# First attention of a four-layer graph stack: scores computed once, products transposed on TensorE

## The chip, the cores and the metric

The kernel runs on one core of a Trainium2 chip. The metric is the time of one execution on the device, in microseconds (us). A core has five engines with a queue each that works strictly in order: PE (TensorE, matrix products; its weight loads are listed as PEld), DVE (VectorE), ACT (ScalarE), POOL (GpSimd) and SP (SyncE, which here only issues DMAs). The engines wait for one another through semaphores. PE writes to PSUM, a memory of banks of 128 partitions x 512 f32.

## The reference

There are 64 independent batch elements, each with `x` (256 nodes x 128 features) and `adj` (256 x 256, some 6% of it nonzero, with the diagonal). Four layers follow one another, each `x = x + layer(relu(layernorm(x)), adj)`: an attention with 8 heads, a one-head graph attention, two graph attention layers with 4 heads each, and a layer that sends a message over every pair of nodes. The change is in the first:

```python
q, k, v = (heads of h @ W.T + b)                    # 8 heads of 16 columns
scores = einsum('bhnd,bhmd->bhnm', q, k) / sqrt(HD)
scores = where(adj == 0, -inf, scores)
attn = softmax(scores, axis=-1) * adj
attn = attn / (attn.sum(-1) + 1e-08)
ctx = einsum('bhnm,bhmd->bhnd', attn, v)            # then @ Wo.T + bo
```

With e = exp(score - row maximum), a context row is sum(e * adj * v) / (sum(e * adj) + 1e-8 * sum(e)). Both kernels compute this form.

## The kernel before

All 64 elements pass through one straight program. Nodes are cut into NB = 2 blocks of 128. The work on an element is split into eight streams, Python generators named by a letter: `f` (`first`: loads, layer norm, the first attention `mha`), `m` (`marks`: masks and ranks), `s` (`second`: the one-head attention and one `gat`), `t` (`third`: the other `gat`), `l` (`lists`: sorted neighbour lists), `e` (`edges`), `g` (`weigh`) and `u` (`fourth`). Each `yield` ends a turn. The string `ORDER` is one round: its letters say which stream takes the next turn. A stream has as many letters in a round as it has turns in an element, so that one round moves every stream on by one element; `START` says by how many rounds and letters a stream lags. In one round the streams thus work on different elements, and the table alone fixes the order of the instructions in every engine's queue. `NBATCH + 9` rounds are run.

Inside `mha`, heads are numbered h = 4a + r with a in 0, 1 and r in 0..3. Head r of group a lies in partitions 32r to 32r + 31 of `qT[:, a]` and `kT[:, a]`: row 0 of the 32 is a spare one, rows 1 to 16 are the head. A product of one head so uses 32 rows of PE, and products of different r can run side by side. The steps of `mha` in the kernel before:

- `qT`, `kT` and values are projected (PE) and copied with bias (ACT, and DVE for the values `va`).
- First pass, queries on partitions: for each block nb and each pair of r, two PSUM banks (from `bank()`, which hands out four) get the mask (`ident_n`, minus 1e30 on its diagonal, times the 0/1 mask) and the scores of two values of a. DVE reduces each bank to row maxima `mx_p` (L468).
- The maxima are transposed by PE (L474), and DVE adds them to the spare rows of `qT` (L476); the spare rows of `kT` hold -1, so that a product is score minus maximum.
- Second pass, keys on partitions: the same products again with swapped operands and the transposed mask; ACT takes the exponential from PSUM to `e` (L491), POOL multiplies by `adT`, the transposed adjacency, into `ew` (L497).
- PE sums over keys into `pc`: `va` (ones and values) by `ew`, and `tiny` (1e-8 in one column) by `e` for the small term. ACT copies `pc` (L511), PE transposes it (L517), DVE divides (L521, L525), and the output projection follows.

Helper `mm` records its products at L408, so its rows are told apart by tiles. In the profile, `ps<-kT,qT` is a product of the first pass and `ps<-qT,kT` one of the second (the moving operand stands first); an f32 product is two MATMUL records, an f32 transpose one. The transposes of the two `gat` stages (L688) are four to a bank, followed by DVE work. The `weigh` stream switches ACT's function table to Gelu and back three times an element (L1020, L1025), the `lists` stream to the square root once (L924, L926).

Of the kernel before, what the change touches and what calls it, by code (L numbers as in the profile page):

```python
# [8 lines left out]
F32 = mybir.dt.float32  # L9
# [27 lines left out]


ORDER = (
    "sggtseffffgegeululeellgfgfggsgltflgfuflfssulfsgulslglfflltgtfgtllggeslgelflslgssglggsflsflftffffssss"  # L40
    "slltllffetefesltstfftllslmeessetftetttgsssftfsefssmffeltutfleselftssfsteeftlffemsustsftmgfslftteggff"
    "tllflflgltlllgfftegfsffesllggmsegfmsleeettfssglgsgllgllletlffsegetfsfttsefffffsfftlsegletlltslselels"
    "tmmllslggugltstgugssuetlgeesgsfllellleellseeusltetlelgggggglstuslstflftslflullsllfgsgsgmfsflllllllll"
    "ltssfgftssffsglllllutlemflg"
)

START = {"f": (0, 17), "s": (1, 17), "t": (2, 9), "l": (3, 29), "e": (5, 1), "u": (6, 11), "g": (5, 23), "m": (0, 0)}
EPS = 1e-5
SLOPE = 0.2
BIG = 1e30  # L50
# [3 lines left out]
def listed_pairs(  # L54
# [82 lines left out]
    V.tensor_copy(ident_b, ident)  # L137
    ident_n = const.tile([P, P], BF16, tag="ident_n", name="ident_n")
    V.tensor_scalar(ident_n, ident, -BIG, None, op0=ALU.mult)
    ones = ct([P, N], "ones")  # L140
    V.memset(ones, 1.0)
    ones_b = const.tile([P, P], BF16, tag="ones_b", name="ones_b")
# [29 lines left out]
        return t, c  # L172

    wq_p, bq_p = by_heads(Wq, bq, 0.0, "wq")
    wk_p, bk_p = by_heads(Wk, bk, -1.0, "wk")
    V.tensor_scalar(bq_p, bq_p, HD ** -0.5, None, op0=ALU.mult)
    wv_t, wo_t = load_t(Wv, "wv"), load_t(Wo, "wo")

    va = ct([P, NB, HEADS, 32], "va")
    V.memset(va, 0.0)  # L180
    V.memset(va[:, :, :, 0:1], 1.0)
    tiny = ct([P, 32], "tiny")
    V.memset(tiny, 0.0)
    V.memset(tiny[:, 0:1], 1e-8)
    mx_p = ct([P, NB, HG, RG, 32], "mx_p")
    V.memset(mx_p, 0.0)
    bv_r, bo_r = load_row(bv, "bv"), load_row(bo, "bo")

    key = const.tile([P, N], I32, tag="key", name="key")
# [228 lines left out]
            mm(p[:, nb, :], hT[:, nb * P:(nb + 1) * P], w)  # L418
        return p

    def mha(hT, adT, xt, mask, maskT, st):


        qT, kT = wt([P, HG, N], "qT", st), wt([P, HG, N], "kT", st)
        p = pt().rearrange("p (a n) -> p a n", a=HG)
        for a in range(HG):
            mm(p[:, a], wq_p[:, a], hT)
        yield
        for a in range(HG):
            S.activation(qT[:, a], p[:, a], AF.Identity, scale=HD ** -0.5, bias=bq_p[:, a:a + 1])  # L430
# [24 lines left out]
        def head(t, r, a, nb=None):  # L455
            return t[32 * r:32 * (r + 1), a, :] if nb is None else t[32 * r:32 * (r + 1), a, nb * P:(nb + 1) * P]

        for nb in range(NB):
            for r in range(0, RG, 2):
                ps = [bank() for _ in range(2)]  # L460
                for j in range(2):
                    mm(ps[j], ident_n, mask[:, nb:nb + 1, :].to_broadcast([P, HG, N]), stop=False)
                for a in range(HG):
                    for j in range(2):
                        mm(ps[j][:, a], head(qT, r + j, a, nb), head(kT, r + j, a), start=False, stop=a == HG - 1)
                yield
                for j in range(2):
                    V.tensor_reduce(mx_p[:, nb, :, r + j, 0], ps[j], axis=AX.X, op=ALU.max)  # L468
                    done("ps")
                    yield  # L470
        pm = pt().rearrange("p (a n) -> p a n", a=HG)
        for nb in range(NB):
            for a in range(HG):
                T.transpose(pm[:, a, nb * P:(nb + 1) * P], mx_p[:, nb, a].rearrange("p r c -> p (r c)"), ident)  # L474
        yield
        V.tensor_tensor(qT, qT, pm, op=ALU.add)  # L476
        done()
        yield
        cn = wt([P, HG, N], "cn", st)
        for nb in range(NB):  # L480
            e = big.tile([P, RG, HG, N], F32, tag="e", name="e", bufs=1)
            for r in range(0, RG, 2):
                ps = [bank() for _ in range(2)]
                for j in range(2):
                    mm(ps[j], ident_n, maskT[:, nb:nb + 1, :].to_broadcast([P, HG, N]), stop=False)
                for a in range(HG):
                    for j in range(2):
                        mm(ps[j][:, a], head(kT, r + j, a, nb), head(qT, r + j, a), start=False, stop=a == HG - 1)
                yield
                for j in range(2):  # L490
                    S.activation(e[:, r + j], ps[j], AF.Exp)  # L491
                    done("ps")
                    yield
            yield
            ew = big.tile([P, RG, HG, N], F32, tag="ew", name="ew", bufs=1)
            for r in range(RG):
                G.tensor_tensor(ew[:, r], e[:, r], adT[:, nb:nb + 1, :].to_broadcast([P, HG, N]), op=ALU.mult)  # L497
                yield
            yield
            if nb == 0:  # L500
                pc = pt("pc").rearrange("p (a n) -> p a n", a=HG)
            for a in range(HG):
                for r in range(RG):
                    mm(pc[32 * r:32 * (r + 1), a, :], tiny, e[:, r, a, :], start=a == 0 and nb == 0, stop=False)
            for a in range(HG):
                for r in range(RG):
                    mm(pc[32 * r:32 * (r + 1), a, :], va[:, nb, a * RG + r, :], ew[:, r, a, :],
                       start=False, stop=a == HG - 1 and nb == NB - 1)
            yield
# [218 lines left out]
    def first(b):  # L728

        xt, ad, adT = x1_[b % 3], ad_[b % 2], adT_[b % 2]  # L730
        if b:
            yield from load_element(b)
        else:
            yield
        if b == min(1, NBATCH - 1):
            for nb in range(NB):
                nc.sync.dma_start(eye_v[:, nb, :], bass.AP(adj.tensor, adj[0].offset + nb * P * (N + 1),
                                                           [[N + 1, P], [N * N, NBATCH], [1, 1]]))
        yield
# [9 lines left out]
        yield from mha(hT, adT, xt, off_[b % 3], offT_[b % 3], "0")  # L749

    def marks(b):

# [958 lines left out]
```

## Time and profile before

| | |
|---|---|
| median of 3 runs | 4637.73 us (4633.71 to 4638.06) |
| profiled execution | 4635.24 us |
| its span (first to last instruction) | 4633.5 us |
| PE busy | 4327.5 us, 93% |
| PE weight loads busy | 2565.2 us, 55% |
| DVE busy | 4027.0 us, 87% |
| ACT busy | 3560.6 us, 77% |
| POOL busy | 2692.4 us, 58% |
| granted PE clock | 0.974 of full speed, mean |

The busy time of an engine is the union of its instructions, in the whole span; the first and last 200 us, in which the streams start and run out, are in it. A row of the groups gives the count, the busy time (union) and the mean duration of one instruction. Where instructions of one engine overlap, busy time divided by count is smaller than the mean duration.

### The profile page before, as it was taken

The numbers are of one execution on the slowest core, as the hardware profiler recorded it, in microseconds if no ns is written. First come the engines' busy times: TensorE is split into PE (matmuls) and PEld (weight loads), VectorE is DVE, ScalarE is ACT, GpSimd is POOL, SyncE is SP. The second block draws the span as 40 slices with busy tenths as digits, with TensorE's granted clock in tenths as the row PEclk, the third lists the DMA queues.
The fourth block names the chain that finished last, engine by engine and source line by source line (L and its number), as shares of the span: only waits on it lengthen the run. The fifth ranks groups of instructions, "written<-read, shape, count | busy, mean of one in ns | idle before, by whom it ended". The sixth has DMA issues, their size and how long they took to land. (4 is left out here: it accounts for less than half of the span.)

```text
span 4633.5 us, 90265 instructions
## 1 busy us (share of the span) xinstructions
PE 4327.5 (93%) x30293; PEld 2565.2 (55%) x30293; DVE 4027.0 (87%) x11727; ACT 3560.6 (77%) x7303; POOL 2692.4 (58%) x3210
## 2 busy tenths in 40 slices
PE   7889999999999999999999999999999999999975
PEld 4455555555555555555555555555555555555543
DVE  4688998998998998898998998998898898898984
ACT  3467878878877878878877877877877877887864
POOL 3345655655665665665665665665665665665644
PEclk8899999999999999999999999999999999999987
DMA  1023444444444444444444444444444443444455
GB/s 27 17 84 114 121 119 119 122 122 117 122 123 116 122 121 118 124 121 117 123 121 117 125 118 116 126 118 115 127 122 111 126 123 110 126 123 110 128 140 134
DMA packets 783433, 533.36 MB, mean 115 GB/s; under 512 B 505321, under 2 KB 678510, under 8 KB 782958
## 3 DMA queue, kind: packets, MB, share of 16 engines
q1 hardware_dynamic: 754286, 493.91, 39.3%
q0 software_dynamic: 28672, 33.58, 3.0%
q8 instruction: 241, 3.95, 0.3%
q14 instruction: 234, 1.92, 0.1%
HBM read 479.47 MB, written 47.84 MB: 114 GB/s over the span
## 5 line engine op out<-in xcount | busy, mean ns | idle before, releaser
L1031 POOL TENSOR_TENSOR ms<-ms,wb 128x512 f32<-128x512 f32 x640 | 832.8, 1401 | 930.3 <-ACT ms L1023 909.3
L497 POOL TENSOR_TENSOR ew<-e,adT 128x512 f32<-128x512 f32 x512 | 639.7, 1268 | 167.6 <-ACT e L491 167.1
L412 PE MATMUL up<-oh,cj 128*128 128x512 f16 x2560 | 658.9, 389 | 22.1 <-DVE oh L982 17.0
L408 PE MATMUL agg<-ms,w2b 128*128 128x256 f32 (+2 forms) x2432 | 650.9, 390 | 12.5 <-POOL ms L1031 12.4
L890 DVE MAX8 best<-pl 128x8 f32<-128x256 f32 x1536 | 620.7, 418 | 16.1
L1006 DVE TENSOR_TENSOR ms<-up,rb 128x512 f32<-128x512 f32 x640 | 434.3, 679 | 187.5 <-PE up L412 133.8
L408 PEld LDWEIGHTS agg<-ms,w2b 128*128 128x128 f32 x2432 | 411.9, 192 | 146.4 <-issue 101.6
L893 DVE MATCH_REPLACE8 pl<-best,pl 128x256 f32<-128x256 f32 x1152 | 470.2, 408 | 0.0
L661 ACT ACTIVATE ps<-ps 128x512 f32<-128x512 f32 x512 | 291.2, 597 | 186.5 <-PE ps L408 186.5
L994 ACT ACTIVATE up<-ci 128x512 f32<-128x512 f32 (+6 forms) x896 | 423.8, 478 | 8.1
L1023 ACT ACTIVATE ms<-ms,be,g 128x1024 f32<-128x1024 f32 x320 | 393.8, 1231 | 14.2 <-DVE ms L1006 13.7
L412 PEld LDWEIGHTS <-cj 128*128 128x128 f16 x2560 | 248.5, 99 | 265.4 <-issue 38.7
L468 DVE TENSOR_REDUCE mx_p<-ps 128x2 f32<-128x512 f32 x512 | 337.8, 682 | 55.4 <-PE ps L408 55.4
L408 PE MATMUL ps<-off,ident_n 128*128 128x512 bf16 x1024 | 318.5, 383 | 40.2 <-DVE mx_p L468 32.6
L670 ACT ACTIVATE y<-ps 128x512 f32<-128x512 f32 x512 | 277.3, 596 | 99.3 <-PE ps L412 99.3
L635 DVE TENSOR_REDUCE m<-ps 128x2 f32<-128x512 f32 x512 | 337.9, 681 | 10.6 <-PE ps L408 10.2
L491 ACT ACTIVATE e<-ps 128x512 f32<-128x512 f32 x512 | 277.7, 594 | 83.0 <-PE ps L408 81.1
L982 DVE TENSOR_SCALAR oh<-cb,code 128x1024 f16<-128x1024 f16 x640 | 337.7, 569 | 0.0
L374 POOL TENSOR_SCALAR rs<-mv 128x2 f32<-128x2 f32 x256 | 79.1, 309 | 410.0 <-DVE mv L367 399.8
L408 PE MATMUL ps<-qT,kT 32*128 32x256 f32 x2048 | 291.9, 402 | 5.8 <-DVE qT L476 1.8
L408 PE MATMUL ps<-kT,qT 32*128 32x256 f32 x2048 | 293.7, 404 | 0.0
L408 PEld LDWEIGHTS ps<-kT,qT 32*128 32x128 f32 x2048 | 176.7, 186 | 165.5 <-issue 151.3
(298 smaller groups left out, 10146.4 us busy)
## 6 DMA issues: line engine op xcount, KB each, us to landing
rb<-ws_d SPq DMA_DIRECT2D x256, 512.0 KB
wb<-ws_d SPq DMA_DIRECT2D x256, 512.0 KB
cb<-code_d SPq DMA_DIRECT2D x256, 256.0 KB
ad<-in_adj_dram SPq DMA_DIRECT2D x64, 256.0 KB
adr<-adr_d SPq DMA_DIRECT2D x64, 256.0 KB
rb<-ws_d SPq DMA_DIRECT2D x64, 168.0 KB
wb<-ws_d SPq DMA_DIRECT2D x64, 168.0 KB
x<-in_x_dram SPq DMA_DIRECT2D x64, 128.0 KB
```

The source lines that it names most:

```text
L408: return T.matmul(o, lhsT=lhsT, rhs=rhs, start=start, stop=stop)
L412: return T.matmul(o, lhsT=lhsT, rhs=rhs, start=False, stop=False, skip_group_check=True)
L468: V.tensor_reduce(mx_p[:, nb, :, r + j, 0], ps[j], axis=AX.X, op=ALU.max)
L497: G.tensor_tensor(ew[:, r], e[:, r], adT[:, nb:nb + 1, :].to_broadcast([P, HG, N]), op=ALU.mult)
L635: V.tensor_reduce(m[:, k + j], ps[j], axis=AX.X, op=ALU.max)
L890: V.max(best[:, n, nb, r:r + 8], planes[n][:, nb])
L893: V.match_replace(planes[n][:, nb], best[:, n, nb, r:r + 8], planes[n][:, nb], 0.0)
L982: V.tensor_scalar(oh[:, jb], cb, code[:, jb:jb + 1], None, op0=ALU.is_equal)
L994: S.activation(ps[:, lo - h * 512:hi - h * 512].rearrange("p (k n) -> p k n", n=cap), ci_[v][:, None, :cap].to_broadcast([P, (hi - lo) // ...
L1006: V.tensor_tensor(ms[:, hs], halves[h], rb[:, hs], op=ALU.mult)
L1023: S.activation(parts[b, c], parts[b, c], AF.Gelu, bias=be1_c, scale=g1_c)
L1031: G.tensor_tensor(ms[:, hs], ms[:, hs], wb[:, hs], op=ALU.mult)
```

## The change

The scores are computed once, with queries on partitions, and negated: `qT` is scaled by -1/sqrt(HD), and the mask is added with `ident_p` (plus 1e30). The row minimum of the negated scores is then the negated maximum, and goes straight into the exponential as its bias: exp(-1 * ps + mn). As the bias differs by block of queries, one exponential covers 128 x 256, and its sum over keys is taken by `accum_out` into `zq`. POOL multiplies by `ad` in place. PE then transposes the products, four 128 x 128 blocks to a bank, ACT copies the bank to `wT`, and the sums with `va` follow. The small term is now added by DVE from `zq`. The order within `mha` is by group a and pair of r: mask and scores, two minima, two turns of two exponentials, two products on POOL, then twice a turn of four transposes and a turn with their copy; after the two pairs of a group, its eight sums. The stream `f` has 81 turns instead of 76. `ORDER` and `START` are new throughout. `adT` is still made, for the masks.

```diff
-START = {"f": (0, 17), "s": (1, 17), "t": (2, 9), "l": (3, 29), "e": (5, 1), "u": (6, 11), "g": (5, 23), "m": (0, 0)}
+START = {"f": (0, 18), "s": (1, 21), "t": (2, 14), "l": (3, 36), "e": (4, 45), "u": (6, 9), "g": (5, 27), "m": (0, 0)}
...
+    ident_p = const.tile([P, P], BF16, tag="ident_p", name="ident_p")
+    V.tensor_scalar(ident_p, ident, BIG, None, op0=ALU.mult)
...
-    wk_p, bk_p = by_heads(Wk, bk, -1.0, "wk")
-    V.tensor_scalar(bq_p, bq_p, HD ** -0.5, None, op0=ALU.mult)
+    wk_p, bk_p = by_heads(Wk, bk, 0.0, "wk")
+    V.tensor_scalar(bq_p, bq_p, -HD ** -0.5, None, op0=ALU.mult)
...
-        for nb in range(NB):
+        mn, zq = sm([P, HG, RG, NB], "mn", st), sm([P, NB, HEADS], "zq", st)
+        cn = wt([P, HG, N], "cn", st)
+        for a in range(HG):
+            wT = big.tile([P, RG, NB, N], F32, tag="wT", name="wT", bufs=1)
             for r in range(0, RG, 2):
+                e = big.tile([P, 2, NB, N], F32, tag="e", name="e", bufs=3)
                 ps = [bank() for _ in range(2)]
                 for j in range(2):
-                    mm(ps[j], ident_n, mask[:, nb:nb + 1, :].to_broadcast([P, HG, N]), stop=False)
-                for a in range(HG):
+                    mm(ps[j], ident_p, mask, stop=False)
+                for nb in range(NB):
                     for j in range(2):
-                        mm(ps[j][:, a], head(qT, r + j, a, nb), head(kT, r + j, a), start=False, stop=a == HG - 1)
+                        mm(ps[j][:, nb], head(qT, r + j, a, nb), head(kT, r + j, a), start=False, stop=nb == NB - 1)
                 yield
                 for j in range(2):
-                    V.tensor_reduce(mx_p[:, nb, :, r + j, 0], ps[j], axis=AX.X, op=ALU.max)
+                    V.tensor_reduce(mn[:, a, r + j], ps[j], axis=AX.X, op=ALU.min)
+                    yield
+                for j in range(2):
+                    for nb in range(NB):
+                        h = a * RG + r + j
+                        S.activation(e[:, j, nb], ps[j][:, nb], AF.Exp, scale=-1.0, bias=mn[:, a, r + j, nb:nb + 1],
+                                     accum_out=zq[:, nb, h:h + 1])
                     done("ps")
                     yield
-        pm = pt().rearrange("p (a n) -> p a n", a=HG)
...
-        V.tensor_tensor(qT, qT, pm, op=ALU.add)
...
-                    mm(ps[j], ident_n, maskT[:, nb:nb + 1, :].to_broadcast([P, HG, N]), stop=False)
-                for a in range(HG):
-                    for j in range(2):
-                        mm(ps[j][:, a], head(kT, r + j, a, nb), head(qT, r + j, a), start=False, stop=a == HG - 1)
-                yield
                 for j in range(2):
-                    S.activation(e[:, r + j], ps[j], AF.Exp)
+                    G.tensor_tensor(e[:, j], e[:, j], ad, op=ALU.mult)
+                    yield
+                for j in range(2):
+                    ps = bank()
+                    for mb in range(NB):
+                        for nb in range(NB):
+                            T.matmul(ps[:, mb, nb * P:(nb + 1) * P], lhsT=e[:, j, nb, mb * P:(mb + 1) * P], rhs=ident,
+                                     is_transpose=True, start=mb == 0 and nb == 0, stop=mb == NB - 1 and nb == NB - 1)
+                    yield
+                    S.activation(wT[:, r + j], ps, AF.Copy)
                     done("ps")
                     yield
...
-                    mm(pc[32 * r:32 * (r + 1), a, :], tiny, e[:, r, a, :], start=a == 0 and nb == 0, stop=False)
...
-                    mm(pc[32 * r:32 * (r + 1), a, :], va[:, nb, a * RG + r, :], ew[:, r, a, :],
-                       start=False, stop=a == HG - 1 and nb == NB - 1)
+                    mm(pc[32 * r:32 * (r + 1), a, :], va[:, mb, a * RG + r, :], wT[:, r, mb, :],
+                       start=a == 0 and mb == 0, stop=a == HG - 1 and mb == NB - 1)
             yield
...
-        V.reciprocal(z, pn[:, :, :, 0])
+        V.scalar_tensor_tensor(z, zq, 1e-8, pn[:, :, :, 0], op0=ALU.mult, op1=ALU.add)
+        yield
+        V.reciprocal(z, z)
```

More of the change, by code (lines that the diff above doesn't have):

```diff
@@ L39 @@
 ORDER = (
[L40 to L44, printed above, removed]
+    "lgsslgesgtssffllllflglllgsffsgggggfuffslssltflggflffglgetgltstlufflllstlelslssegfgggsfegstufsffgttfs"
+    "gggsssfffsssggfsffetlltslellfsetstletmlsleflstlllsststssfetmfuusftflteffusfffffsfgtftfgtmffflelsgsge"
+    "mseetellsfetteltslttteelgettfggfegegegeglslggflgltftlfflltelffmelutssssfggtsmtgsfttllllllslfsltflsgl"
+    "fsttfllsmllfslftftfeulsftfeesfelesfeelmestlsslgglulggeeeegfsllleggsffleelfslfgsllflfstfsslslfssffffg"
+    "lgmggeeeetluulllllllululumlllltl"
 )
-START = {"f": (0, 17), "s": (1, 17), "t": (2, 9), "l": (3, 29), "e": (5, 1), "u": (6, 11), "g": (5, 23), "m": (0, 0)}
+START = {"f": (0, 18), "s": (1, 21), "t": (2, 14), "l": (3, 36), "e": (4, 45), "u": (6, 9), "g": (5, 27), "m": (0, 0)}
 EPS = 1e-5
@@ L181, in listed_pairs @@
     V.memset(va[:, :, :, 0:1], 1.0)
[L182 to L186, printed above, removed]
     bv_r, bo_r = load_row(bv, "bv"), load_row(bo, "bo")
@@ L419, in tokens, with mha @@
         return p
-    def mha(hT, adT, xt, mask, maskT, st):
+    def mha(hT, ad, xt, mask, st):
         qT, kT = wt([P, HG, N], "qT", st), wt([P, HG, N], "kT", st)
@@ L429, in mha @@
         for a in range(HG):
-            S.activation(qT[:, a], p[:, a], AF.Identity, scale=HD ** -0.5, bias=bq_p[:, a:a + 1])
+            S.activation(qT[:, a], p[:, a], AF.Identity, scale=-HD ** -0.5, bias=bq_p[:, a:a + 1])
             if a == HG - 1:
@@ L469, in mha @@
                     done("ps")
                     yield
-        pm = pt().rearrange("p (a n) -> p a n", a=HG)
-        for nb in range(NB):
-            for a in range(HG):
-                T.transpose(pm[:, a, nb * P:(nb + 1) * P], mx_p[:, nb, a].rearrange("p r c -> p (r c)"), ident)
-        yield
[L476 to L483, printed above, removed]
-                for j in range(2):
-                    mm(ps[j], ident_n, maskT[:, nb:nb + 1, :].to_broadcast([P, HG, N]), stop=False)
-                for a in range(HG):
-                    for j in range(2):
-                        mm(ps[j][:, a], head(kT, r + j, a, nb), head(qT, r + j, a), start=False, stop=a == HG - 1)
-                yield
-                for j in range(2):
-                    S.activation(e[:, r + j], ps[j], AF.Exp)
+                for j in range(2):
+                    G.tensor_tensor(e[:, j], e[:, j], ad, op=ALU.mult)
+                    yield
@@ L493, in mha @@
                     yield
[L494 to L500, printed above, removed]
+            if a == 0:
                 pc = pt("pc").rearrange("p (a n) -> p a n", a=HG)
-            for a in range(HG):
+            for mb in range(NB):
                 for r in range(RG):
-                    mm(pc[32 * r:32 * (r + 1), a, :], tiny, e[:, r, a, :], start=a == 0 and nb == 0, stop=False)
@@ L505, in mha @@
-            for a in range(HG):
-                for r in range(RG):
-                    mm(pc[32 * r:32 * (r + 1), a, :], va[:, nb, a * RG + r, :], ew[:, r, a, :],
-                       start=False, stop=a == HG - 1 and nb == NB - 1)
-            yield
+                    mm(pc[32 * r:32 * (r + 1), a, :], va[:, mb, a * RG + r, :], wT[:, r, mb, :],
+                       start=a == 0 and mb == 0, stop=a == HG - 1 and mb == NB - 1)
             yield
@@ L748, in first @@
         hT = yield from ln_relu_t(xt, "0")
-        yield from mha(hT, adT, xt, off_[b % 3], offT_[b % 3], "0")
+        yield from mha(hT, ad, xt, off_[b % 3], "0")
     def marks(b):
```

## The prediction

> **What bounds the kernel now.** First the page's busy shares, then the busy time of each engine in one round, because shares of the whole span mix in the fill and the drain. A round is found in the timeline of ACT: the same Gelu instruction, preceded by its table load, comes back after 2067.91 - 1998.98 = 68.93 us.
>
> ```profile
> PE 4327.5 (93%) x30293; PEld 2565.2 (55%) x30293; DVE 4027.0 (87%) x11727; ACT 3560.6 (77%) x7303; POOL 2692.4 (58%) x3210
> ...
> 1998.98 1.23 ACT L1023 ACTIVATE ms<-ms,be,g 128x1024 f32<-128x1024 f32 x1
> ...
> 2067.91 1.23 ACT L1023 ACTIVATE ms<-ms,be,g 128x1024 f32<-128x1024 f32 x1
> ...
> 1998.98:2067.91 68.93, 66.21 (x475) 39.34 (x473) 62.32 (x182) 55.45 (x115) 42.04 (x51) 1.00 0.46 121
> ```
>
> The last line gives the round: PE busy 66.2 of 68.93 us (96.1%), DVE 62.3 (90.4%), ACT 55.45 (80.4%), POOL 42.0 (61%). PE is the bound and idles 2.7 us a round. The waits say the same from the other side: what ACT waits for is mostly PE.
>
> ```profile
> ACT ps L661 <- PE ps L408: 186.5, 66, 5.6
> ACT cjT L848 <- PE pt L408: 112.8, 61, 2.5
> ACT nd L682 <- PE pt L408: 106.6, 67, 4.8
> ACT y L670 <- PE ps L412: 99.3, 131, 2.7
> ACT cj L834 <- PE pt L408: 87.8, 63, 2.0
> ACT e L491 <- PE ps L408: 81.1, 183, 13.2
> ```
>
> These six are 674 us, or 10.5 of ACT's 13.5 us of idle a round. The chain that ended last covers only the drain and says nothing of the round. So the sum is made per round, engine by engine, and multiplied by 63 rounds; fill and drain (4633.5 - 63 x 68.93 = 291 us) I leave as they are, since `f` alone sets neither.
>
> **PE.** Removed: the second pass, the small term, the transposes of the maxima. Added: 32 transposes (8 heads x 4 blocks). The mask and scores of the first pass and the sums with `va` stay in number and shape. The groups by form:
>
> ```profile
> L408 PE MATMUL ps<-qT,kT 32*128 32x256 f32 x2048 | 291.9, 402 | 5.8 <-DVE qT L476 1.8
> L408 PE MATMUL ps<-offT,ident_n 128*128 128x512 bf16 x512 | 156.0, 384 | 1.2 <-ACT e L491 0.8
> L408 PE MATMUL pc<-e,tiny 128*32 128x256 f32 x2048 | 140.0, 387 | 0.2
> L688 PE MATMUL pt<-ident,nd 128*128 128x128 f32 x512 | 77.2, 273 | 1.3 <-ACT nd L682 1.3
> L474 PE MATMUL pt<-ident,mx_p 128*128 128x128 f32 x256 | 39.2, 275 | 0.3 <-DVE mx_p L468 0.3
> ```
>
> By busy time, (291.9 + 156.0 + 140.0 + 39.2) / 64 = 9.8 us go. The nearest row to the new transposes is L688: f32, 128 x 128, four to a bank. 77.2 / 512 = 0.151 us each, 32 make 4.8. Net -5.0. By the distance of starts in the timeline it is the same: a second pass of two banks takes 1.60 us, sixteen small-term products 0.88, and
>
> ```profile
> 2003.47 0.60 PE L688 MATMUL pt<-ident,nd 128*128 128x128 f32 x4
> 2003.90 0.38 PE L1059 MATMUL pt<-ident,ag 128*128 128x128 f32 x2
> ```
>
> four transposes 0.43: 4 x 1.60 + 2 x 0.88 + 0.44 = 8.6 go and 8 x 0.43 = 3.4 come, -5.2. If each transpose cost its whole mean duration, 32 x 0.273 = 8.7, the net would be -1.1. I take -5.0, as four in a row are what L688 shows: PE 61.2 (at worst 65.1).
>
> Here a rule speaks against the change. The Trainium skill ("TensorE: Matmul & The Clock Gate", Part 4) gives about 275 ns for a transpose inside a kernel and says that transposes do not count as busy for the clock gate. The row agrees with the duration (273 ns) but the starts are 0.11 us apart, and the round with its transposes has a granted clock of 1.00. By the rule as a price PE would end at about 65 us; by the row it ends at 61.2.
>
> **ACT.** Removed: 8 exponentials of 128 x 512 from PSUM, busy 277.7 / 64 = 4.3 us. Added: 8 copies of 128 x 512 from PSUM (L682: 0.588 us, starts 0.50 apart; 4.0 to 4.7, taken 4.4) and 16 exponentials of 128 x 256 with bias and accumulated sum. The same form, from SBUF, is in the one-head attention:
>
> ```profile
> 2038.10 0.51 ACT L574 ACTIVATE lo<-lo,mx 128x256 f32<-128x256 f32 x1 [0.41 <-DVE mx L570]
> 2038.51 0.19 ACT L574 ACTIVATION_READ_ACCUMULATOR lo<-lo,mx 128x1 f32 x1
> 2038.61 0.49 ACT L574 ACTIVATE lo<-lo,mx 128x256 f32<-128x256 f32 x1
> ```
>
> The accumulated sum is an instruction of its own, but its 0.19 us overlaps both neighbours: one exponential starts 0.51 us after the other. 16 x 0.51 = 8.2 us; without overlap 16 x (0.500 + 0.187) = 11.0. Net: +7.9 at least, +11.4 at most; I take 8.2 + 4.4 - 4.3 = +8.3, since the turns hold two exponentials in a row as that row does. ACT goes from 55.45 to 63.7 and becomes the fullest engine. Replaying the letters of the new table against the turns, no turn with an exponential falls between a switch to Gelu and the switch back, so the eight table loads (1.28 us each) stay eight.
>
> **DVE.** The reductions stay (8 of 128 x 512, 0.682 us; minimum instead of maximum). The addition to `qT` goes (43.3 / 64 = 0.68), a step of 16 columns comes (L639, 128 x 8: 0.24). Net -0.4: 61.9.
>
> **POOL.** 8 products as before; in place they cost between 1.268 (L497) and 1.401 us (L1031, in place, same size), at most +1.1 on an engine at 42 of 69 us, hidden. No DMA is added or removed, and loads keep their streams.
>
> **The chain within `f`.** New waits: an exponential waits for its minimum, a transpose for POOL, `wT` (one buffer) for the sums of the group before. What queues behind them is all other streams' work on ACT and PE. A pair of heads now takes, one after the other, 1.60 (scores) + 1.36 (minima) + 2.04 (exponentials) + 2.54 (POOL) + 2.04 (transposes, copies) = 9.6 us, four of them 38 us. In the table this stretch has 276 of 432 letters, 43 us of a 67.6 us round. Before, the same stretch summed to 37.5 us (passes 11.8 + 10.8, maxima 1.1, POOL 10.1, sums 3.7) and had 251 of 427 letters, 40.5 us. So the chain is not tighter than it was, and I cost it at nothing as long as the others fill the gaps; if they do not, rival 2 is its price.
>
> **The sum.** After: ACT 63.7, DVE 61.9, PE 61.2. The round follows from how full the fullest engine can be. At PE's share now (96.1%) it is 66.3 us, at that of the second fullest now (DVE, 90.4%) 70.5. I go a third of the way down, to 94.2%, nearer to the first because 10.5 of ACT's 13.5 us of idle ended with the PE that is now relieved, but not to it, because three engines lie within 2.5 us: 63.7 / 0.942 = 67.6 us. That is -1.33 x 63 = -84 us: 4635.2 - 84 = 4551 for the profiled execution, and, as that lies 2.5 us below the median, **4554 us** beside 4637.7. Its own range has ACT's net at +7.9 and a share of 96.1% at one end (65.9 us a round, 4447) and 68.4 us a round (4604) at the other.
>
> **Rivals.**
> 1. ACT becomes the bound to the point of loss. The place is the 16 exponentials: if reading the accumulator does not overlap, ACT's net is +11.4, it reaches 66.8, and at 94.2% the round is 70.9 us: +124, **4762**. It decides from a net of about +9.5 on, that is when an exponential with its sum takes 0.58 us instead of 0.51. For it: the two rows' busy times (64.0 and 23.9 us for 128 each) add to 0.69 us. Against it: the starts above.
> 2. Idle time is kept, not work: today PE, DVE and ACT idle 3 x 68.93 - 184.0 = 22.8 us together. If the waits between engines that cause it stay, the round is (186.8 + 22.8) / 3 = 69.9 us: +61, **4699**. For it: three nearly full engines in strict order, and a chain that passes through four engines four times a round. Against it: most of ACT's idle was PE's lateness.
> 3. DVE, not ACT, holds the round, with its share of 90.4%: 61.9 / 0.904 = 68.5 us, -27, **4611**. For it: DVE has long runs in `l` that nothing else shortens. Against it: DVE too waits for PE now (133.8 us at L1006, 55.4 at L468).
>
> **How the numbers follow.** What a measurement of this kernel can tell from no change is about 0.2%, or 9 us. Forecast 0.50; rival 1 0.21; rival 2 0.20; rival 3 0.09. Rivals 2 and 3 spread about their values so that 0.02 of each lies within 9 us of no change. Faster 0.50 + 0.07 = 0.57; same 0.04; slower 0.21 + 0.18 = 0.39. The range runs from the forecast's lower end to rival 1: 4450 to 4765, which leaves out some 0.1 at each end. The likeliest case alone: 4447 to 4604.
>
> **What would show it.** In the changed profile, a round of 67.6 us with ACT busy near 63.7, PE near 61.2, DVE near 61.9; 2048 transposes of the products with some 310 us busy; 1024 further accumulator reads of 0.19 us, and exponentials that start 0.51 us apart; 512 copies near 0.59 us; ACT's waits for PE well under 674 us. I am wrong if ACT is over 65.5 us busy a round (rival 1), if all three engines idle over 6.5 us a round (rival 2), or if PE stays above 64 us, because the transposes follow one another at more than 0.2 us.

## The result, and the profile after

Before 4637.41 us, after 4645.29 us (medians of 20 runs each): a ratio of 1.0016, with a 95% interval of 1.0009 to 1.0023. That is 8 us more: the interval leaves out 1, but the change is inside the 0.2% that the prediction counts as no change. The time lies in the forecast's range, but the forecast itself, 4554 us, is 91 us away. The profiled execution took 4641.65 us, of which 4639.8 are its span.

The page's shares come first, then the two Gelu starts that bound one round and the sum of the busy times between them (columns after the length: PE, PEld, DVE, ACT, POOL).

```profile
PE 4133.7 (89%) x27285; PEld 2565.9 (55%) x27477; DVE 3918.2 (84%) x11725; ACT 4003.4 (86%) x9351; POOL 2764.1 (60%) x3210
...
1999.07 1.23 ACT L1012 ACTIVATE ms<-ms,be,g 128x1024 f32<-128x1024 f32 x1
...
2067.95 1.23 ACT L1012 ACTIVATE ms<-ms,be,g 128x1024 f32<-128x1024 f32 x1
...
sum 68.88, PE 63.01 PEld 39.30 DVE 60.45 ACT 62.30 POOL 43.16; mean PE 4.50 PEld 2.81 DVE 4.32 ACT 4.45 POOL 3.08
```

This round is 68.88 us where before it was 68.93. Over many rounds the same Gelu start gives 69.12 us after (315.92 to 4048.32, 54 rounds) and 69.19 before (313.70 to 4050.09): 63 x -0.07 = -4 us. Fill and drain are 285 us after (4639.8 - 63 x 69.12) and 274.5 before: +11. Together they make the 6 us by which the two profiled spans differ. So the round stayed as long, though PE lost 3.2 us of work, DVE 1.9, and ACT gained 6.9. PE, DVE and ACT idle 3 x 68.88 - 185.76 = 20.9 us a round together; before it was 22.8. PE's own idle time grew from 2.7 to 5.9 us and DVE's from 6.6 to 8.4, while ACT's fell from 13.5 to 6.6: where work left PE and DVE, waiting took its place.

Half of the waiting stands in one place. These are two neighbouring slices of 4.92 us of the round after, then the two at the same place before (columns: slice, length, then busy time and count of PE, PEld, DVE, ACT, POOL, then granted clock, DMA share, GB/s).

```profile
2023.67:2028.59 4.92, 2.88 (x23) 2.37 (x20) 4.71 (x20) 2.59 (x7) 4.12 (x11) 1.00 0.12 40
2028.59:2033.51 4.92, 3.34 (x11) 2.54 (x12) 1.22 (x3) 3.87 (x8) 2.96 (x6) 0.72 0.53 173
```

```profile
2023.60:2028.52 4.92, 3.63 (x26) 2.68 (x25) 3.53 (x14) 4.83 (x10) 3.95 (x8) 1.00 0.08 25
2028.52:2033.44 4.92, 4.42 (x24) 3.43 (x23) 3.08 (x8) 4.64 (x14) 3.32 (x6) 1.00 0.11 32
```

In these 9.84 us PE, ACT and DVE are busy 6.22, 6.46 and 5.93 us and idle 10.9 together; before they idled 5.4 there. In the remaining 59.04 us they idle 10.0 after and 17.4 before, and are 96.2%, 94.6% and 92.3% full. Outside this place the change did what it was costed at. Here it lost 5.5 us of the idle time that it gained elsewhere. I call the place the join, because three streams come to their layer norms there: `t`, `s` and `f`. The waits say what for (engine, line, tile, releaser: total, times, longest). After:

```profile
ACT xn L381 <- POOL nm L374: 225.4, 135, 5.4
...
DVE pair L917 <- ACT pair L913: 215.3, 63, 4.9
PE pt L389 <- ACT xn L381: 212.7, 129, 2.9
```

Before:

```profile
POOL rs L374 <- DVE mv L367: 399.8, 70, 19.8
...
ACT xn L384 <- POOL nm L377: 33.1, 66, 8.0
...
PE pt L392 <- ACT xn L384: 25.8, 48, 2.9
...
DVE pair L928 <- ACT pair L924: 1.1, 2, 0.6
```

Before, POOL waited for the statistics; after, ACT waits for POOL, PE for ACT, and DVE (L917, the reciprocal of the lists) for ACT's square root, which stands behind the norms in ACT's queue. The timeline of POOL shows why (start, length). After:

```profile
2024.04 0.49 POOL L371 TENSOR_SCALAR rs<-mv 128x2 f32<-128x2 f32 x1
2024.62 0.72 POOL L372 TENSOR_TENSOR rs<-rs,m_half 128x2 f32<-128x2 f32 x1
...
2026.00 0.22 POOL L371 TENSOR_SCALAR rs<-mv 128x2 f32<-128x2 f32 x1
...
2027.67 0.22 POOL L371 TENSOR_SCALAR rs<-mv 128x2 f32<-128x2 f32 x1
2027.98 1.27 POOL L372 TENSOR_TENSOR rs<-rs,m_half 128x2 f32<-128x2 f32 x1
...
2029.63 0.20 POOL L374 TENSOR_TENSOR nm<-nm,rs 128x2 f32<-128x2 f32 x1
```

Before (the last operation of `t`'s norm, then the first of the other two):

```profile
2020.58 0.20 POOL L377 TENSOR_TENSOR nm<-nm,rs 128x2 f32<-128x2 f32 x1
...
2026.65 0.22 POOL L374 TENSOR_SCALAR rs<-mv 128x2 f32<-128x2 f32 x1
...
2028.36 0.22 POOL L374 TENSOR_SCALAR rs<-mv 128x2 f32<-128x2 f32 x1
```

After the change the norms of `t`, `s` and `f` pass through POOL one behind another, 1.6 to 2.2 us each; four operations on two columns take that long. The third is the longest because its power takes 1.27 us instead of 0.71; DVE runs `oh` from 2028.00 to 2028.88, beside it. Before, `t`'s was done at 2020.78, six microseconds ahead of the other two. Letters of the table are counted from 0 here. In the table before, the norms' turns are letters 31 (`t`), 95 (`f`) and 100 (`s`), and the square root is letter 86, ahead of `f`'s and `s`'s; in the new one the norms are 89 (`t`), 108 (`f`) and 105 (`s`), and the square root is letter 127, behind them all.

The wait has a second price, in PE's clock. The timeline of PE:

```profile
2028.17 0.71 PE L389 MATMUL pt<-ident,xn 128*128 128x128 f32 x2 [1.98 <-ACT xn L381]
2030.41 0.86 PE L389 MATMUL pt<-ident,xn 128*128 128x128 f32 x2 [1.52 <-ACT xn L381]
```

It waits 1.98 and 1.52 us for `xn` with one pair of transposes in between, and the granted clock is 0.72 in the second slice above and 0.93 in the one behind it. The groups of after:

```profile
L389 PE MATMUL pt<-ident,xn 128*128 128x128 f32 x384 | 125.3, 368 | 216.1 <-ACT xn L381 212.7
...
L405 PE MATMUL pt<-hT,wsnd 128*128 128x256 f32 x256 | 116.7, 609 | 0.0
```

and of before:

```profile
L392 PE MATMUL pt<-ident,xn 128*128 128x128 f32 x384 | 99.3, 320 | 28.5 <-ACT xn L384 25.8
...
L408 PE MATMUL pt<-hT,wsnd 128*128 128x256 f32 x256 | 66.8, 384 | 0.0
```

The same products take 609 ns instead of 384. With the products `wpre,hT` (78.5 us busy instead of 40.3) that is 26.0 + 49.9 + 38.2 = 114 us, 1.8 us a round: about what PE has over the 61.2 us forecast. Smaller changes in other rows go both ways (the products `up<-oh,cj`, 24.0 us less; the sums with `va`, 17.4 more).

### The profile page after: what moved, and what is told of

Same layout as the page of the kernel before. It is cut to its first block, busy times and chain, and to the rows that moved or that the text cites. A ratio compares the mean times of both kernels' runs of the same rounds, so it can differ in the third digit from the quotient of the medians.

```text
span 4639.8 us, 87431 instructions
## 1 busy us (share of the span) xinstructions
PE 4133.7 (89%) x27285; PEld 2565.9 (55%) x27477; DVE 3918.2 (84%) x11725; ACT 4003.4 (86%) x9351; POOL 2764.1 (60%) x3210
## 5 line engine op out<-in xcount | busy, mean ns | idle before, releaser
L479 POOL TENSOR_TENSOR e<-e,ad 128x512 f32<-128x512 f32 x512 | 678.1, 1334 | 720.7 <-ACT e L474 577.2
L1020 POOL TENSOR_TENSOR ms<-ms,wb 128x512 f32<-128x512 f32 x640 | 808.2, 1282 | 288.8 <-ACT ms L1012 273.1
L474 ACT ACTIVATE e<-ps,mn 128x256 f32<-128x256 f32 x1024 | 473.9, 480 | 65.6 <-DVE mn L469 59.0
L381 ACT ACTIVATE xn<-x,nm,rs 128x128 f32<-128x128 f32 x512 | 224.8, 489 | 228.0 <-POOL nm L374 225.4
L469 DVE TENSOR_REDUCE mn<-ps 128x2 f32<-128x512 f32 x512 | 335.3, 686 | 90.7 <-PE ps L405 86.1
L485 PE MATMUL ps<-ident,e 128*128 128x128 f32 x2048 | 305.8, 283 | 58.7 <-POOL e L479 57.6
L1071 POOL DMA_INDIRECT x<-ur_d,rank x128 | 212.7, 1661 | 216.1 <-PE pt L405 122.9
L488 ACT ACTIVATE wT<-ps 128x512 f32<-128x512 f32 x512 | 293.4, 601 | 32.2 <-PE ps L485 23.8
L389 PE MATMUL pt<-ident,xn 128*128 128x128 f32 x384 | 125.3, 368 | 216.1 <-ACT xn L381 212.7
L485 PEld LDWEIGHTS ps<-ident,e 128*128 128x128 f32 x2048 | 238.6, 144 | 127.9 <-POOL e L479 96.6
```

Source lines behind the costliest of these rows:

```text
L474: S.activation(e[:, j, nb], ps[j][:, nb], AF.Exp, scale=-1.0, bias=mn[:, a, r + j, nb:nb + 1], accum_out=zq[:, nb, h:h + 1])
L479: G.tensor_tensor(e[:, j], e[:, j], ad, op=ALU.mult)
L485: T.matmul(ps[:, mb, nb * P:(nb + 1) * P], lhsT=e[:, j, nb, mb * P:(mb + 1) * P], rhs=ident, is_transpose=True, start=mb == 0 and nb == 0, ...
L1020: G.tensor_tensor(ms[:, hs], ms[:, hs], wb[:, hs], op=ALU.mult)
```

## The experiments

The theory from these readings, M in the texts on record: the round is held at the join by the norms on POOL and by what queues behind them, and the table put them there. Against it stood that one engine's load holds the round after all, and that the waits would move elsewhere if these went. Ratios are to the kernel before, run beside.

**`t`'s norm taken earlier.** One letter moves 18 places towards the front.

```diff
-...lllstlelssegfgggsfegstufsffgttfs"
+...lllsttlelssegfgggsfegsufsffgttfs"
```

> The changed kernel with one letter of the table moved: the turn of stream t that holds its layer norm's statistics and its four POOL steps comes right after t's addition, 18 letters earlier. No instruction is added or left out. Theory M (in the changed round three layer norms meet on POOL at the join of f's end and s's start, some 2 us each, while ACT and PE wait): the norms of s and f start up to 2 us earlier, the round falls by 1 to 2 us, 4520 to 4580 us. Rival A (ACT's load holds the round): within 10 us of 4645. Rival I (idle time only moves about): within 20 us of 4645, the stretch is shorter and others longer.

Measured: 4770.85 us, 1.0288 (1.0274 to 1.0302): a miss. The norm now stands on POOL ahead of other work and waits for its input, with everything behind it:

```profile
PE pt L389 <- DVE o L695: 165.4, 64, 5.1
ACT g1T L391 <- PE pt L389: 164.4, 64, 2.8
POOL rs L371 <- DVE over L895: 161.7, 62, 2.7
```

The letter moved alone changes two queues at once: DVE's, with the statistics, and POOL's, with the four operations. This says nothing against the join, but does against mending it by hand.

**A shorter norm on POOL.** In `one_over_std`, two of the four operations go to DVE, so that POOL keeps the power and one product.

```diff
-        G.tensor_scalar(rs, mv[:, :, 1], EPS, None, op0=ALU.add)
+        V.tensor_scalar(rs, mv[:, :, 1], EPS, None, op0=ALU.add)
+        V.tensor_scalar(nm, mv[:, :, 0], -1.0, None, op0=ALU.mult)
         G.tensor_tensor(rs, rs, m_half, op=ALU.pow)
-        G.tensor_scalar(nm, mv[:, :, 0], -1.0, None, op0=ALU.mult)
         G.tensor_tensor(nm, nm, rs, op=ALU.mult)
```

> The changed kernel with the layer norms of f, s and t shorter on POOL: the addition of epsilon and the sign of the mean go to DVE (two steps of two columns, about 0.15 us each), POOL keeps the power and one product. POOL's part of a norm falls from about 2.0 to 1.1 us, DVE gets up to 1.2 us a round. Theory M: three norms in a row are shorter by 2.7 us, the round by 1 to 2.5 us: 4490 to 4580 us. Rival A: no change, within 10 us of 4645. Rival I: 0 to 60 us more, for DVE's eight added steps.

Measured: 4552.22 us, 0.9822 (0.9808 to 0.9835), 93 us under the change as it was.

```profile
ACT xn L381 <- POOL nm L374: 107.7, 72, 5.0
```

The wait for POOL is half as long. The round, over 55 rounds, is 67.60 us (306.71 to 4024.92), 1.52 less, and 63 x 1.52 = 96 us is the whole gain. DVE is busier by 132 us (4050.7 against 3918.2). Part of POOL's relief was not in the edit: the power, which stays, falls from 889 to 716 ns in the mean, as none is stretched at its new time.

**The same in the kernel before,** as control.

> The same edit of the layer norms in the kernel before. There POOL waited for DVE at the norms (400 us in all) and ACT waited only 33 us for POOL's result. All theories: within 25 us of 4637; if the edit is worth as much here as in the changed kernel, theory M falls.

Measured: 4668.57 us, 1.0068 (1.0054 to 1.0082). There the edit costs 32 us, a little over the 25 expected at most: DVE gets 122 us more work (4148.9 against 4027.0 busy), and POOL, which waited 399.8 us for DVE's statistics, waits 413.3 for the end of the two operations that moved. So the gain belongs to the norms as they stand in the changed kernel, not to the norm as such.

**No accumulated sum.** The exponential drops `accum_out`, and `zq` holds ones.

```diff
-                        S.activation(e[:, j, nb], ps[j][:, nb], AF.Exp, scale=-1.0, bias=mn[:, a, r + j, nb:nb + 1],
-                                     accum_out=zq[:, nb, h:h + 1])
+                        S.activation(e[:, j, nb], ps[j][:, nb], AF.Exp, scale=-1.0, bias=mn[:, a, r + j, nb:nb + 1])
```

> The changed kernel without the accumulated sums of the 16 exponentials (the sum of exponentials in the 1e-8 term is replaced by 1). ACT loses 16 accumulator reads, which in the trace put 0.455 us instead of about 0.36 between two exponentials: 1.5 us a round. Rival A: the round falls by the whole 1.5 us, 4550 us. Theory M: the stretch with the norms stays as it is, the rest, where ACT is 94% busy, shortens by 0.5 to 1.5 us: 4550 to 4615. Rival I: within 20 us of 4645.

Measured: 4735.05 us, 1.0213 (1.0199 to 1.0226): 90 us more with less work, which no theory had. The join's waits are as they were (225.8, 218.8 and 217.7 us). What grew are two rows of DVE, here without the sum and below it as in the change:

```profile
L972 DVE TENSOR_SCALAR oh<-cb,code 128x1024 f16<-128x1024 f16 x640 | 406.2, 676 | 0.6 <-DMA cb<-code_d 0.6
...
L875 DVE TENSOR_TENSOR pl<-ad,pm 128x512 int32<-128x512 int32 x64 | 105.8, 1653 | 2.2
```

```profile
L971 DVE TENSOR_SCALAR oh<-cb,code 128x1024 f16<-128x1024 f16 x640 | 344.6, 580 | 0.5 <-DMA cb<-code_d 0.5
...
L874 DVE TENSOR_TENSOR pl<-ad,pm 128x512 int32<-128x512 int32 x64 | 45.2, 706 | 2.2
```

Together +122 us, 1.9 us a round, on operations that the edit does not touch. `e` reaches POOL at other times, and POOL's products then lie beside other DVE operations: here `pl` starts at 2023.64, 0.13 us after a POOL product of 1.27 us, and takes 1.68 us. In the change it starts at 2057.22 between two such products and takes 0.69, and the product that starts 0.23 us after it takes 1.60 instead of 1.27. The Trainium skill ("SBUF — State Buffer", "SBUF: two separate sides") says that DVE and GpSimd share a port pair which one instruction holds to its end, on DVE's side one with two SBUF inputs or in a 2-port mode. The times of `pl`, which has two SBUF inputs, agree with that; no run here shows the mode of `oh`, which has one tensor input. As a test of the sum's cost the run is void. That the longer rows are what cost the 90 us is not shown: 91 us less of other DVE work returned 7 us (below).

**The old attention in the new table.** The kernel before, with the new `ORDER` and `START` and empty turns where the new attention has more (two behind the addition to `qT`, three more after the first sums and one fewer after the second, one after the reciprocal).

```diff
-ORDER = ...   # and START, of the kernel before
+ORDER = ...   # and START, of the change
...
+        yield     # empty turns
```

> The attention of the kernel before, run by the new ORDER and START (five empty turns added to f so that the head, the last sums and the tail of f stand at the same letters as in the changed kernel; the middle is spread over the letters between). If the meeting of the layer norms at the join comes from the new table: ACT waits for POOL's nm and PE for xn over 150 us each here too, and with PE's 66 us of work the round is over 70 us, 4700 us or more. If it comes from the new work of the attention: those two waits stay under 60 us each (33 and 26 in the kernel before).

Measured: 5287.93 us, 1.1404 (1.1385 to 1.1423). The size says little, as this table does not fit the old steps inside `f` (ACT's exponentials wait 290.3 us for PE, against 81.1). But the join's waits are there, with none of the new work:

```profile
ACT xn L384 <- POOL nm L377: 226.7, 137, 5.6
...
DVE pair L935 <- ACT pair L931: 215.3, 63, 4.9
```

225.4 and 215.3 us in the change, 226.7 and 215.3 here: they come with the table.

**Less work on one engine,** three kernels. In the third plane of the lists DVE searches only the first of the two blocks; ACT copies the first half of each transposed bank; PE does not add the mask.

```diff
# less DVE
-                    V.max(best[:, n, nb, r:r + 8], planes[n][:, nb])
+                    if n < 2 or nb == 0:
+                        V.max(best[:, n, nb, r:r + 8], planes[n][:, nb])    # match_replace likewise
# less ACT
-                    S.activation(wT[:, r + j], ps, AF.Copy)
+                    S.activation(wT[:, r + j, 0], ps[:, 0], AF.Copy)
# less PE
-                for j in range(2):
-                    mm(ps[j], ident_p, mask, stop=False)
...               # the scores of block 0 then start the bank
```

> The changed kernel with DVE relieved outside f and outside the join: the sorted lists leave out the third bit plane of the second block (3 MAX8, 2 MATCH_REPLACE8 with their value loads: 3 x 0.42 + 2 x 0.50 = 2.2 us a round). Theory D (away from the join DVE holds the round: it idles only 2.8 of 59 us there): 1.4 to 2.2 us less, 4505 to 4560 us. Theory A (ACT holds it) and theory P (PE holds it): within 25 us of 4645.

> The changed kernel with half of each copy to wT left out (128 x 256 instead of 128 x 512, the other half of wT stays at 1): ACT loses 8 x 0.21 = 1.7 us a round. Theory A: 1.3 to 1.7 us less, 4540 to 4565 us. Theories D and P: within 30 us of 4645; more if DVE's steps that read two SBUF tiles get into POOL's way, as in the run without sums, where oh and pl took 1.9 us more a round.

> The changed kernel without the mask products of the first attention's scores (all pairs of nodes count): PE loses 8 x 0.29 = 2.3 us a round. Theory P: 1.5 to 2.3 us less, 4500 to 4550 us. Theories D and A: within 30 us of 4645.

Measured: DVE busy 91 us less in the page, time 4638.04 us (1.0002, 0.9992 to 1.0011), 7 us under the change. ACT 100 us less, 4619.34 us (0.9969, 0.9957 to 0.9980), 26 under. PE 90 us less (the row left out had 149.5), 4588.01 us (0.9898, 0.9881 to 0.9914), 57 under. ACT's wait for `nm` stays at 220.4, 229.3 and 222.5 us. No single engine's load returns its own size; the two operations of the short norm, which take no work away, returned 93.

**`t`'s norm taken later,** behind the others: its letter and the two that follow in `t` move behind letter 108.

```diff
-...segfgggsfegstufsffgttfs" "gggsssfffsssggfsffet...
+...segfgggsfegsufsffgfsggg" "sssffftsssggfsfttfet...
```

> The changed kernel with three letters of the table moved: stream t's norm (its statistics with the POOL steps, and its two normalising turns on ACT) comes after the norms of s and f instead of before them. No instruction is added or left out. Theory M (s and f wait at the join because POOL works through t's norm first): s and f start up to 2 us earlier, the round falls by 1 to 2 us: 4520 to 4585 us. Rival R (what s and f wait for at the join is the end of f's own tail, and POOL's order adds nothing): within 20 us of 4645.

Measured: 4702.08 us, 1.0139 (1.0122 to 1.0156): a miss. ACT's wait for `nm` fell to 116.3 us, but `s`'s copy `hT` now stands on ACT behind `t`'s normalisation, and PE waits for it:

```profile
PE pt L405 <- ACT hT L391: 122.3, 92, 2.2
```

**POOL's addition of the bias earlier.** In `mha`, `xt` + `bo` moves from the end to the turns after `va`, leaving an empty place; alone, and with the short norm.

```diff
+        G.tensor_tensor(xt, xt, rows(bo_r), op=ALU.add)    # after the va turns
...
-        G.tensor_tensor(xt, xt, rows(bo_r), op=ALU.add)    # after cT
```

> The changed kernel with POOL's addition of the output bias to x (0.73 us, just ahead of the norms at the join) done earlier in f, after the values, where POOL idles. The turns stay. Theory M: 0.3 to 0.7 us less a round, 4600 to 4625 us. Rival R: within 10 us of 4645.

> The changed kernel with both the short norm on POOL and the early bias. Theory M: up to 0.7 us a round under the short norm alone (4552): 4505 to 4550 us. Rival R: 4552, within 10 us.

Measured: 4660.38 us (1.0054, 1.0037 to 1.0070) and 4586.17 us (0.9891, 0.9875 to 0.9908): 15 us over the change and 34 over the short norm, both misses. Two rows of DVE grew again. With both edits:

```profile
L606 DVE TENSOR_SCALAR yt<-x,lane 128x256 bf16<-128x256 f32 x128 | 73.0, 571 | 0.0
L604 DVE TENSOR_SCALAR ys<-x,lane 128x256 bf16<-128x256 f32 x128 | 66.2, 517 | 0.1
```

They took 450 and 404 ns in the change: +30 us, and +25 with the early bias alone (593 and 460 ns). The moved addition itself took 1367 ns, and 1325 with the early bias alone, instead of 729.

**PE kept busy in the wait.** Ahead of the transposes of `s`'s and `f`'s `xn`, PE gets five and four idle products into the bank that the transposes then overwrite.

```diff
+        for _ in range(fill):                                  # in transposed(); 5 for s, 4 for f
+            T.matmul(p, lhsT=ones_b, rhs=fill_b, start=True, stop=True)
```

> The changed kernel with PE kept at work at the join: nine products of ones (128 x 512 bf16, some 0.25 us each) ahead of the transposes of s's first norm and f's norm, overwritten by these. In the changed kernel the granted clock is 0.72 in the slice after these waits, and the products with wsnd and wpre take 609 and 462 ns instead of 384 and 281. Theory C (the lower clock after the wait is a good part of what the join costs): these products are back at 384 and 281 ns, the round falls by 0.5 to 1.3 us: 4560 to 4615 us. Theory M alone: the products are faster but their users wait for POOL anyway: within 20 us of 4645.

Measured: 4624.15 us, 0.9975 (0.9964 to 0.9985), 21 us under the change.

```profile
L391 PE MATMUL pt<-fill_b,ones_b 128*128 128x512 bf16 x512 | 146.1, 388 | 3.8 <-issue 0.4
...
L409 PE MATMUL pt<-hT,wsnd 128*128 128x256 f32 x256 | 72.8, 411 | 0.0
```

The nine products, 0.285 us each by their row (512 of the 576 are in the trace), bring `wsnd` back from 609 to 411 ns and the mean clock from 0.944 to 0.977. ACT still waits 225.9 us for `nm`. So the clock is a price on top of the wait, and 21 of the 91 us that were missed come back.

**The join put in another order by hand,** alone and with the short norm: letters 89 to 142 permuted so that `s` and `f` come first and `t` follows.

```diff
-...segfgggsfegstufsffgttfs" "gggsssfffsssggfsffetlltslellfsetstletmlslef...
+...segfgggsfegsufsffgfsggg" "sssfflftlllsssggsssffffsfsllttteeettttemlle...
```

> The changed kernel with 60 letters of the table at the join in another order and nothing else changed: t's norm on POOL after those of s and f, and its normalising turns on ACT later still; s's transposed copy and its first product ahead of f's normalising turns; the square root of the lists prepared earlier on DVE and POOL. Theory T (the dead time at the join is a property of the table, which orders t's and f's steps ahead of s's on POOL, ACT and PE in turn): s's first product starts 1.5 to 2.5 us sooner after f's last addition, and the round falls by 1 to 2.5 us: 4490 to 4585 us. Theory W (the join costs what it costs, because three chains end and start there at once; a step put first puts another last, as in the two runs that moved t's letters alone): 4645 or more.

> The same order with the short norm on POOL. Theory T: the two add in part, 4440 to 4530 us. Theory W: 4552 or more, as the short norm alone gave.

Measured: 4684.31 us (1.0099, 1.0083 to 1.0114) and 4667.09 us (1.0067, 1.0053 to 1.0080). The first order all but removes ACT's wait for `nm` (7.2 us instead of 225.4) and more than halves PE's for `xn` (83.9), and the kernel is slower all the same: the total of a wait is not its price. The waits moved: `lo` of `s` stands on ACT behind `t`'s normalisation, and the low clock now falls on `f`'s query products, which took 385 ns in the change. In the first of the two:

```profile
DVE lo L555 <- ACT lo L550: 148.8, 64, 2.4
```

```profile
L405 PE MATMUL pt<-hT,wq 128*128 128x256 f32 x256 | 95.3, 508 | 33.7 <-ACT rows L927 33.2 <-ACT hT L391 0.5
```

**No norm on POOL at all,** in both kernels. The statistics are taken, but scale and bias are constants.

```diff
-        rs, nm = one_over_std(stats(t, st), st)
+        stats(t, st)
+        rs, nm = ones, m_half
```

> The changed kernel with POOL's four steps left out of the norms of f, s and t (x is scaled by 1 and shifted by -0.5 instead; the statistics on DVE stay). Theory M (the join's dead time is POOL working through three norms): ACT's wait for nm and most of PE's wait for xn are gone, the round falls by 2 to 3.5 us, 4425 to 4520 us. If it falls by less than the 93 us of the short norm, POOL is not what the join costs.

> The same left out of the kernel before, as a control: there ACT waited 33 us for POOL's nm in all, so 0 to 45 us less, 4592 to 4637 us. If it falls by as much as the changed kernel does, theory M falls.

Measured: 4530.05 us (0.9767, 0.9752 to 0.9782) and 4593.54 us (0.9901, 0.9885 to 0.9916). The edit brings 115 us in the changed kernel and 44 in the kernel before, 71 us less; these two differ in table and attention, and the run with the old attention in the new table is what ties the waits to the table. A little more was expected (4520 us or less).

```profile
PE pt L390 <- ACT xn L382: 84.9, 122, 1.2
...
DVE pair L918 <- ACT pair L914: 65.9, 61, 3.2
```

PE still waits for `xn` and DVE for the square root, so POOL is most of the join, not all.

**The short norm with PE kept busy,** and the idle products alone in the kernel before.

> The changed kernel with the short norm and with the nine products that keep PE at work ahead of the transposes of the norms. Theory C (the clock after the wait has a price of its own, 21 us in the changed kernel): 4520 to 4545 us. Without it: 4552 or more, as the wait to be filled is shorter here.

> The same nine products in the kernel before, as a control. Its granted clock is 0.99 to 1.00 in the rounds and PE is its bound: nothing to gain, up to 9 x 0.25 = 2.2 us a round to lose, 4637 to 4780 us. If it gains, the products do something other than holding the clock.

Measured: 4529.73 us, 0.9770 (0.9757 to 0.9784), and 4723.59 us, 1.0181 (1.0166 to 1.0197). Before, where PE is 93% busy, nine products cost 86 us. In the new table with the short norm they gain 22:

```profile
PE 4132.5 (91%) x27858; PEld 2508.3 (55%) x28053; DVE 4035.4 (89%) x12238; ACT 3997.2 (88%) x9351; POOL 2619.2 (58%) x2698
```

DVE stands at 89% instead of 84% and the round at 67.37 us (305.27 to 4010.79, 55 rounds). This version is 2.3% faster than the kernel before and 2.5% faster than the change (4529.73 / 4645.29 = 0.975).

## Why the prediction was right and wrong

**Right: the price of each new operation.** The transposes cost what the nearest row said, and the accumulated sum overlaps its neighbours. PE's load came out above its term all the same, for another reason (below). After:

```profile
L485 PE MATMUL ps<-ident,e 128*128 128x128 f32 x2048 | 305.8, 283 | 58.7 <-POOL e L479 57.6
```

```profile
2007.68 0.48 ACT L474 ACTIVATE e<-ps,mn 128x256 f32<-128x256 f32 x1
2008.04 0.21 ACT L474 ACTIVATION_READ_ACCUMULATOR e<-ps,mn 128x1 f32 x1
2008.13 0.48 ACT L474 ACTIVATE e<-ps,mn 128x256 f32<-128x256 f32 x1
```

305.8 / 2048 = 0.149 us against 0.151 forecast; one exponential starts 0.45 us after another against 0.51, and not the 0.58 from which rival 1 would decide. The copies were 293.4 / 512 = 0.573 us; the table loads stayed 512. ACT's load came out at 62.3 us, not 63.7: the exponentials account for 16 x 0.06 = 1.0 of it. DVE's was 60.45, not 61.9: 0.9 of it is the row `mrows`, 82.6 us busy before and 23.8 after, which fell from 646 to 186 ns an instruction; its code is the same and only its place is new. `f`'s chain cost little: its largest new waits on PE and ACT are 57.6 us (PE for POOL's product) and 59.0 us (ACT for the minima), under a microsecond a round each.

**Wrong: "The sum".** The loads forecast add up to 186.8 us and those measured to 185.8, which is partly luck: PE was 1.8 us over its term, ACT and DVE 1.4 each under. The step that failed is the one that makes a round of it: one share, 94.2%, for the whole round. Over 59 of 68.9 us that share was right (ACT 94.6% full); the other 9.84 us were taken to be like the rest, and there ACT is 66% full (6.46 us). Over the whole round ACT is 90.4% full; at 94.2% its 62.3 us would have made a round of 66.1. The prediction put the effect of the new table at nothing, and had looked in it only for Gelu windows and for the length of `f`'s chain. The table is an edit of its own, and it changed the order of three norms and a square root. The old attention in the new table shows the same waits; the short norm, which touches nothing but the norms, brings the round to 67.60 us. That this is just the round forecast is chance: the edit gives DVE more work, and leaves waits of 107.7, 91.0 and 32.7 us at the join.

**Mis-sized by this: PE's term,** 63.0 us instead of 61.2. Most of the 1.8 us is a lower clock after the waits, on products that the change leaves as they were. The prediction did weigh a rule on the clock, but for the transposes, and not for PE's new idle time. The Trainium skill ("TensorE: Matmul & The Clock Gate", "Why this matters for your kernels") warns of gaps over about 3 us; here gaps of 1.98 and 1.52 us with transposes between them were followed by the lower clock. Its Part 4, that transposes do not count as busy the same way, would agree with that, but no run here parts the gaps from the transposes.

**The rivals.** Rival 2, idle time is kept, is nearest: 22.8 us were forecast to stay and 20.9 did. With the measured loads its formula gives (185.8 + 22.8) / 3 = 69.5 us a round; this one was 68.9. But its reason, a general lateness of engines in strict order, was not the mechanism: outside one place idle time fell, from 17.4 to 10.0 us. Rival 1 needed ACT over 65.5 us busy; it had 62.3. Rival 3 falls with the less-DVE run (91 us less of DVE, 7 us less of time). The sign by which the prediction called itself wrong, all three idle over 6.5 us a round, was met nearly: PE 5.9, DVE 8.4, ACT 6.6.

**Fill and drain** were forecast unchanged and grew by 11 us, against -4 us in the rounds. The new `START` and the shape of the first turns were not costed; no run took this apart.

**Open.** Whether an order exists in which the new attention runs without the join: three tables changed by hand, and the one operation moved in `mha`, were all slower. How the loss at the join parts between POOL's norms and the square root behind them: the runs that shortened the first also shortened the wait for the second.

## What to carry to other kernels

A new order of instructions is a change by itself: before pricing it, look in it for places where short serial chains of several streams come to one in-order engine, and ask what stands behind them in every other queue. The loads of the engines were forecast within 3% here, and their sum within 1%, and the time was still missed by 2%, since a round is the busy stretches plus the joins. A wait was paid twice where the clock fell after it, and a few idle products in the wait were cheaper than the slow products behind it (21 and 22 us gained), but only where the engine did wait (86 us lost in the kernel before).

## What the runs showed of the hardware that was not expected

- PE waits of 1.98 and 1.52 us within 4.2 us, with one pair of transposes between, were followed by a granted clock of 0.72, and by products of 609 ns instead of 384.
- DVE operations that the edits did not touch changed by up to 2.3 times when work was moved elsewhere: `pl` (int32, 128 x 512) 706 to 1653 ns, `oh` 580 to 676, `yt` 450 to 593.
- Less work made the kernel slower: without the accumulated sums, 90 us more.
- Four POOL operations on 128 x 2 elements take 1.6 to 2.2 us; the power alone 0.71 to 1.27, the longest one beside a DVE operation.
